# One matmul for centre and gate in two steps of eight, and one pair of PSUM buffers for both

## The chip, the cores and the metric

The kernel runs on one core of a Trainium2 chip. The metric is the device time of one execution in microseconds (us), lower is better. The engines are named as in the profile: PE is TensorE's matmul and PEld its weight load, DVE is VectorE, ACT is ScalarE, POOL is GpSimd, and SP issues DMAs. PE's results land in tiles of PSUM, which lie in banks, and DVE and ACT read them there. Everything is fp32.

## The reference, cut to what matters

The input `x` is an image of 512 x 512 pixels with 64 channels. Layer 0 is a triangle product with an output gate, layer 1 a spectral convolution; each is added to its input.

```python
xn  = _ln(x, norm_w, norm_b)                        # x is group-normed before
...
out_gate = sigmoid(xn @ ogate_w + ogate_b)          # (1, 512, 512, 64)
out = einsum('bkjd,bkid->bijd', left, right)        # masked and gated sides
out = _ln(out, onorm_w, onorm_b) @ out_w + out_b
x   = x + out * out_gate                            # layer 0
x   = x + ifft2(w * fft2(_gn(x))[12 x 12 modes])    # layer 1
```

The change is in `out_gate` alone. The kernel takes the layer norm in front of it apart: one matmul with `center_x` gives the centred pixels (their squares, summed over 64 channels, give the variance), another with `gate_x` gives the unscaled gate, and the gate is multiplied afterwards with the reciprocal standard deviation of its pixel.

## The kernel before, in words

Only at most 256 of the 512 rows are left by the mask, and the function `compact` works on those. After the statistics, the projections and the triangle product, it runs one long hand-ordered loop over steps `s` (L1193). Eight steps make a **unit** (`SIZE`). The first eight units (`k < first`) turn the triangle product into normed rows `u_d`; I call them the product stage. Then come 32 **output units**, `v = 0 .. 31`, each 128 rows by 64 pixels, and the change is about these. `manual_schedule` keeps every engine's instructions in the order of the source, and waits are put in from the tiles that instructions read and write.

In step `s`, with `n = s % 8`, the engines do this, in the order in which each has it:

- PE transposes four 128 x 128 blocks of step `s + 13` (`t_ps`, L1038), takes the gate of step `s` (`w_ps`, four matmuls of `times`, L1045) and then the centred pixels of step `s + 12` (`c_ps`, also L1045). In the steps with n = 0 and 4 the column transform (`f_ps`, L1140) follows. One fp32 matmul of the source is two instructions in the trace.
- ACT copies the transposed pixels to SBUF (`xt_c`, L1040); in even steps it takes the sigmoid of the gate that DVE finished in the step before (`z_t`, L1221); in the step n = 5 it takes the square root for the next unit (`rs_n`, L1089); last it squares the centred pixels of step `s + 12` (`sq_c`, L1076). In the trace one `ACT_TABLE_LOAD` stands ahead of the square root and one ahead of the next sigmoid.
- DVE takes four statistics of the finished unit (`stats2c`, L1168); in even steps it sums the squares of two steps (`scratch`, L1083); at n = 7 it takes the reciprocal of 64 standard deviations (L1263); then it multiplies the gate of step `s` with its factor (`z_t<-w_ps,rs_n`, L1274), and in odd steps it adds the gate's bias to the pair of steps (L1280). I write "multiplication(n)" and "add(n)" for the last two. In every fourth unit from v = 5 on, the steps n = 2 and 4 hold five more DVE instructions that join statistics (L1173 to L1186, and L230); I call these the join units.
- POOL multiplies the sigmoid with the normed row (L1109) and adds it to the pixels (L1113), each 128 x 1024 once in two steps, and issues two gathers a unit.

The PSUM tiles of the output stage are two buffers of one bank for `c_ps` and two of one bank for `w_ps`. They take the place of the two `y_ps` buffers (two banks each) of the product stage, which are closed when step 52 begins (L1206). In the product stage a tile `both` holds two 64 x 64 matrices beside each other in both halves of its partitions, and the matmul of L1058 takes 64 channels at a time, from the upper or the lower half: the results of a channel half are the centred pixels in the first 64 columns and the projected ones in the other 64. ACT squares the first (L1078) and copies the second to SBUF (L1079). `scratch` is one PSUM tile for sums of squares (`totals`), for the product stage's reciprocals (`factors`) and for biases.

## Time and profile before

| what | us |
|---|---|
| median of three runs (lowest, highest) | 1777.96 (1777.58, 1781.21) |
| the profiled execution, its time | 1777.78 |
| span of its trace, first to last instruction | 1776.0 |
| busy: PE, DVE, POOL, ACT | 1567.8, 1413.7, 936.5, 933.0 |
| product stage, first to last matmul of L1058 | 624.6 to 728.9 |
| first and last `c_ps` matmul | 730.5 to 1415.6 |
| first and last `w_ps` matmul | 747.8 to 1443.5 |

The chain of work that ended last is, from 1469 us to the end, the spectral layer and the DMAs that store the output; it does not reach back to the output units. So their pace is read from the trace itself: I cut it at the reciprocal that stands ahead of multiplication(7) (L1263), which gives one stretch for each unit. A line of the profile's groups gives the source line, the engine, what is written and read, the count, the busy time, the mean of one in ns, and behind the second bar the idle time of the engine just before them with what ended it. A line of the timeline gives start and duration in us, the engine, the line and, in brackets, the idle time before it.

### The profile page before, as it was taken

The page shows a single profiled execution, that of the slowest core. Times are in us where ns is not written, and L with a number is a line of the kernel's source. Part 1 is how long each engine was busy: PE and PEld are TensorE (multiplying, and loading weights), DVE is VectorE, ACT ScalarE, POOL GpSimd, SP SyncE. Part 2 cuts the span into 40 slices and gives each one's busy share as a digit, 9 for nine tenths or more (in the row PEclk, how much of TensorE's full clock was granted, in tenths as well). Part 3 has the DMA queues.
Part 4 walks back from the last instruction along what each step waited for, and adds up shares of the span by engine and source line. Part 5 has one row for each costly group of instructions (what it writes and reads, how often), then busy time and mean ns, then how long its engine had stood idle before and what let it go on. Part 6 is the DMA issues. An engine that isn't in the chain of part 4 may idle for free. (4 is left out here: it accounts for less than half of the span.)

```text
span 1776.0 us, 32619 instructions
## 1 busy us (share of the span) xinstructions
PE 1567.8 (88%) x10918; PEld 1242.0 (70%) x10918; DVE 1413.7 (80%) x2982; ACT 933.0 (53%) x1660; POOL 936.5 (53%) x695
## 2 busy tenths in 40 slices
PE   6779799997999978899999999999999977998772
PEld 5667666662899867787888888888888745665341
DVE  7989678887455568688999999999999984865451
ACT  3666566663333266676777777777777742011000
POOL 4666211111000037698999999999999881111110
PEclk9999999999899999899999999999999976555555
DMA  7999278878898789868767767776776699999999
GB/s 281 386 386 388 107 206 227 229 229 245 279 305 303 257 246 347 298 196 296 265 242 257 253 233 259 264 249 239 249 264 244 212 318 400 425 427 427 426 427 385
DMA packets 192593, 518.48 MB, mean 292 GB/s; under 512 B 37664, under 2 KB 104480, under 8 KB 151456
## 3 DMA queue, kind: packets, MB, share of 16 engines
q1 hardware_dynamic: 156112, 295.65, 47.5%
q0 software_dynamic: 32832, 218.45, 33.4%
q10 hardware_dynamic: 3472, 2.20, 0.5%
q8 instruction: 89, 1.46, 0.3%
q14 instruction: 88, 0.72, 0.1%
HBM read 311.60 MB, written 204.60 MB: 291 GB/s over the span
## 5 line engine op out<-in xcount | busy, mean ns | idle before, releaser
L1045 PE MATMUL w_ps<-gate_x,xt_c 128*128 128x128 f32 x2048 | 280.5, 281 | 30.0 <-DVE z_t L1274 28.6
L1113 POOL TENSOR_TENSOR places<-places,z_t 128x1024 f32<-128x1024 f32 x127 | 301.3, 2372 | 8.0
L1045 PEld LDWEIGHTS w_ps<-gate_x,xt_c 128*128 128x128 f32 x2048 | 252.0, 194 | 46.4 <-DVE z_t L1274 44.6
L1045 PE MATMUL c_ps<-center_x,xt_c 128*128 128x128 f32 x2048 | 277.0, 279 | 0.8 <-ACT xt_c L1040 0.4
L1045 PEld LDWEIGHTS c_ps<-center_x,xt_c 128*128 128x128 f32 x2048 | 252.8, 194 | 3.8 <-ACT xt_c L1040 3.0
L1440 PE MATMUL l_ps<-places,rinv 24*128 24x512 f32 x512 | 206.2, 1118 | 29.3 <-DVE places L1447 19.0
L1168 DVE BATCH_NORM_STATS2 stats2c<-places 128x6 f32<-128x128 f32 x1024 | 220.5, 278 | 9.9 <-POOL places L1113 9.9
L1083 DVE TENSOR_REDUCE scratch<-sq_c 128x16 f32<-128x1024 f32 x160 | 194.6, 1216 | 31.1 <-ACT sq_c L1078 16.1
L1221 ACT ACTIVATE z_t<-z_t 128x1024 f32<-128x1024 f32 x128 | 135.5, 1058 | 131.8 <-DVE z_t L1280 131.1
L1440 PEld LDWEIGHTS l_ps<-places,rinv 24*128 24x128 f32 x512 | 119.8, 302 | 110.8 <-DVE places L1447 56.9
L1278 POOL TENSOR_TENSOR z_t<-z_t,bias_row_out 128x1024 f32<-128x1024 f32 x32 | 75.6, 2363 | 226.3 <-PE y_ps L1058 202.1
L1040 ACT ACTIVATE xt_c<-t_ps,ab_xc 128x512 f32<-128x512 f32 x256 | 176.0, 688 | 11.5 <-PE t_ps L1038 10.6
L1274 DVE TENSOR_TENSOR z_t<-w_ps,rs_n 128x512 f32<-128x512 f32 x256 | 172.0, 672 | 6.2 <-PE w_ps L1045 6.1
L1076 ACT ACTIVATE sq_c<-c_ps 128x512 f32<-128x512 f32 x256 | 150.8, 589 | 31.4 <-PE c_ps L1045 30.8
L1280 DVE TENSOR_TENSOR z_t<-z_t,scratch 128x1024 f32<-128x1024 f32 x128 | 156.3, 1221 | 9.9 <-ACT rs_n L1089 3.7
L688 DVE BATCH_NORM_STATS2 stats1c<-x_ps 128x6 f32<-128x512 f32 x256 | 157.1, 682 | 7.7 <-PE x_ps L687 7.4
L1109 POOL TENSOR_TENSOR z_t<-z_t,places 128x1024 f32<-128x1024 f32 x64 | 151.8, 2371 | 14.6 <-ACT z_t L1221 14.4
L1038 PE MATMUL t_ps<-c_ident,places 128*128 128x128 f32 x1024 | 158.4, 278 | 0.0
L1038 PEld LDWEIGHTS t_ps<-c_ident,places 128*128 128x128 f32 x1024 | 118.5, 142 | 51.4 <-issue 51.4
L1447 DVE TENSOR_TENSOR places<-places,l_ps 128x512 f32<-128x512 f32 x176 | 109.3, 682 | 55.2 <-DMA places<-x_h,dst_i 42.1
L1109 POOL TENSOR_TENSOR z_t<-z_t,bias_row_out 128x1024 f32<-128x1024 f32 x63 | 149.4, 2372 | 5.8 <-ACT z_t L1221 5.5
L673 ACT COPY xc<-xg 128x128 f32 x352 | 105.0, 298 | 66.1 <-POOL xc L673 47.1
(214 smaller groups left out, 2557.0 us busy)
## 6 DMA issues: line engine op xcount, KB each, us to landing
x_h<-places SPq DMA_DIRECT2D x64, 1024.0 KB
out_x<-places SPq DMA_DIRECT2D x44, 1024.0 KB
places<-u_d SPq DMA_DIRECT2D x512, 64.0 KB
out_x<-lx_t SPq DMA_DIRECT2D x20, 1024.0 KB
rbc<-rs_d POOLq DMA_DIRECT2D x32, 512.0 KB, 7.1
left_d<-o_c SPq DMA_DIRECT2D x64, 256.0 KB
right_d<-o_c SPq DMA_DIRECT2D x64, 256.0 KB
left_raw<-left_d SPq DMA_DIRECT2D x64, 256.0 KB
```

What stands on the lines that cost most here:

```text
L688: nc.vector.bn_stats(stats[:, 0, 16 * (jc % quarter) + 4 * r + c, :], ps.rearrange("p i k -> p (i k)"))
L1038: nc.tensor.transpose(tps[:, i, :], flat[:, o : o + P], ident)
L1040: nc.scalar.activation(xts[s], tps, AF.Identity, bias=ab1[:, 2:3])
L1045: nc.tensor.matmul(ps[:, 2 * i : 2 * i + 2, :], xts[s][:, i, :], w, start=True, stop=True)
L1076: nc.scalar.activation(sq, cps, AF.Square)
L1083: nc.vector.tensor_reduce(totals[k % 2][:, 8 * (n - 1) : 8 * (n + 1)], sqs.pop(s // 2), AX.X, ALU.add)
L1109: nc.gpsimd.tensor_mul(zs[k, c], zs[k, c], u)
L1113: nc.gpsimd.tensor_add(xr, xr, zs.pop((k, c)))
L1168: nc.vector.bn_stats(st[k // 4][:, g, k % 4, :], x_of(k)[:, :, 2 * g : 2 * g + 2])
L1274: nc.vector.tensor_mul(z[:, 8 * odd : 8 * odd + 8, :], wps, rs)
L1280: nc.vector.tensor_add(z, z, bias_ps["ogate"].unsqueeze(1).to_broadcast([P, 16, C]))
L1440: nc.tensor.matmul(ps.rearrange("p j o -> p (j o)"), rinv[h, b, :], it[h], start=True, stop=True, tile_position=(32 * g, 0),)
```

## The change

The tile `both`, which only the product stage used, is filled a second time when step 52 begins: the two diagonal blocks of `center_x` and of `gate_x`. In the output units, the steps with `s % 4 == 0` (n = 0 and 4) are called joint. For a joint step the centred pixels and the gate come from eight matmuls of 64 channels each, at the place where the centred pixels alone were made, that is 12 steps before the gate is needed. ACT squares the centred half and copies the gate half to SBUF, over the transposed pixels. Twelve steps later DVE reads the gate from there.

The other six steps make the centred pixels and the gate with the same matmuls as before, in the same order. But the `y_ps` buffers now stay open: each step takes one tile of two banks, with the centred pixels of step `s + 12` in the first bank and the gate of step `s` in the second. There are two such tiles.

The reciprocals of a unit are taken in two instructions: 16 of them, for the joint steps, go to `factors` in the PSUM tile `scratch`, and 48 stay in SBUF. The multiplication of a joint step so reads its gate from SBUF and its factor from PSUM; in the other steps it is the other way round, as before.

```diff
+                    def joint(s):
+                        return s >= first * SIZE and s % 4 == 0
+                    def times(bank, s, w):
                         for i in range(4):
+                            nc.tensor.matmul(bank[:, i, :], xts[s][:, i, :], w, start=True, stop=True)
+                        return bank.rearrange("p i (h c) -> p (i h) c", h=2)
...
+                    def centered(s, ps):
+                        if joint(s):
+                            for i in range(4):
+                                for h in range(2):
+                                    hs = slice(h * C, (h + 1) * C)
+                                    nc.tensor.matmul(ps[:, h, i, :], xts[s][hs, i, :], both[hs], start=True, stop=True)
+                            return ps
                         if s >= first * SIZE:
-                            return times(ps_c, "c_ps", s, center_x)
+                            return times(ps[:, 0], s, center_x)
...
-                        if s >= first * SIZE:
+                        if joint(s):
+                            nc.scalar.activation(in_order(sq), cps[:, :, :, :C], AF.Square)
+                            kept = xts[s].rearrange("p i (h c) -> p (i h) c", h=2)
+                            nc.scalar.copy(in_order(kept), cps[:, :, :, C:])
+                        elif s >= first * SIZE:
                             nc.scalar.activation(sq, cps, AF.Square)
...
                         if s + LEAD - 1 == first * SIZE:
-                            products.close()
-                            ps_c = products.enter_context(tc.tile_pool(name="np_c", bufs=2, space=PSUM))
-                            ps_w = products.enter_context(tc.tile_pool(name="np_w", bufs=2, space=PSUM))
+                            for h in range(2):
+                                hs = slice(h * C, (h + 1) * C)
+                                nc.vector.tensor_copy(both[hs, :C], center_x[hs, hs])
+                                nc.vector.tensor_copy(both[hs, C:], gate_x[hs, hs])
+                        if s + LEAD - 1 >= 0 and s < total_g:
+                            ps = ps_y.tile([P, 2, 4, P], F32, name="y_ps")
                         if 0 <= s < total_g:
-                            wps = raw(s) if k < first else times(ps_w, "w_ps", s, gate_x)
+                            if k < first:
+                                wps = raw(s)
+                            elif joint(s):
+                                wps = xts[s].rearrange("p i (h c) -> p (i h) c", h=2)
+                            else:
+                                wps = times(ps[:, 1], s, gate_x)
...
-                            nc.vector.reciprocal(factors[(k + 1) % 2] if k + 1 < first else rss[k + 1], rss[k + 1])
+                            if k + 1 < first:
+                                nc.vector.reciprocal(factors[(k + 1) % 2], rss[k + 1])
+                            else:
+                                by = [t.rearrange("p (a b) -> p a b", a=2) for t in (factors[(k + 1) % 2], rss[k + 1])]
+                                nc.vector.reciprocal(by[0][:, :, :8], by[1][:, :, :8])
+                                nc.vector.reciprocal(by[1][:, :, 8:], by[1][:, :, 8:])
...
-                                rs = rss[k][:, 8 * n : 8 * n + 8].unsqueeze(2).to_broadcast([P, 8, C])
+                                rs = (factors[k % 2] if joint(s) else rss[k])[:, 8 * n : 8 * n + 8]
+                                rs = rs.unsqueeze(2).to_broadcast([P, 8, C])
```

The function `finished`, which multiplies the last two gates of all in PSUM, takes one `y_ps` tile in place of two `c_ps` tiles.

More of the change, by code (lines that the diff above doesn't have):

```diff
@@ L996, in compact @@
                     ps_y = products.enter_context(tc.tile_pool(name="np_b", bufs=2, space=PSUM))
-                    ps_c = ps_w = None
                     both = lp.tile([P, P], F32, name="both")
@@ L1040, in transpose @@
                         nc.scalar.activation(xts[s], tps, AF.Identity, bias=ab1[:, 2:3])
-                    def times(pool, name, s, w):
-                        ps = pool.tile([P, 8, C], F32, name=name)
+                    def joint(s):
+                        return s >= first * SIZE and s % 4 == 0
+                    def times(bank, s, w):
                         for i in range(4):
-                            nc.tensor.matmul(ps[:, 2 * i : 2 * i + 2, :], xts[s][:, i, :], w, start=True, stop=True)
-                        return ps
-                    def centered(s):
+                            nc.tensor.matmul(bank[:, i, :], xts[s][:, i, :], w, start=True, stop=True)
[7 more added lines that the diff above has]
+                            return ps
                         if s >= first * SIZE:
-                            return times(ps_c, "c_ps", s, center_x)
-                        ps = ps_y.tile([P, 2, 4, P], F32, name="y_ps")
+                            return times(ps[:, 0], s, center_x)
                         q, e = divmod(s, 2)
@@ L1064, in raw, with in_order @@
                         return xts[s].rearrange("p h (i c) -> p (h i) c", c=C).rearrange("p (h i) c -> p h i c", h=2)
+                    def in_order(t):
+                        return t.rearrange("p (i h) c -> p h i c", h=2)
                     def of_pair(t, e):
@@ L1117, in finished @@
                         z = zs.pop((last, 3))
-                        made = [ps_c.tile([P, 8, C], F32, name="c_ps") for _ in range(2)]
+                        made = ps_y.tile([P, 2, 4, P], F32, name="y_ps")
+                        made = [made[:, i].rearrange("p i (h c) -> p (i h) c", h=2) for i in range(2)]
                         for i, ps in enumerate(made):
@@ L1206, in compact @@
                         if s + LEAD - 1 == first * SIZE:
-                            products.close()
-                            ps_c = products.enter_context(tc.tile_pool(name="np_c", bufs=2, space=PSUM))
-                            ps_w = products.enter_context(tc.tile_pool(name="np_w", bufs=2, space=PSUM))
-                        if 0 <= s < total_g:
-                            wps = raw(s) if k < first else times(ps_w, "w_ps", s, gate_x)
-                            del xts[s]
+                            for h in range(2):
[4 more added lines that the diff above has]
+                            ps = ps_y.tile([P, 2, 4, P], F32, name="y_ps")
+                        if 0 <= s < total_g:
+                            if k < first:
[4 more added lines that the diff above has]
+                                wps = times(ps[:, 1], s, gate_x)
                         if 0 <= s + LEAD - 1 < total_g:
-                            cps = centered(s + LEAD - 1)
+                            cps = centered(s + LEAD - 1, ps)
                         if n in (0, 4) and held(1):
@@ L1287, in compact @@
                                     zs[v, c] = z
+                        xts.pop(s, None)
                         if n == 7 and held(0) and v < last:
```

## The prediction

> **What bounds the kernel now.** The change touches only the output units, so I read their stretch. On the profile's page I look at the two operations that meet there, PE's gate matmul and DVE's multiplication, and at the idle time behind their second bar.

> ```profile
> L1045 PE MATMUL w_ps<-gate_x,xt_c 128*128 128x128 f32 x2048 | 280.5, 281 | 30.0 <-DVE z_t L1274 28.6
> ...
> L1274 DVE TENSOR_TENSOR z_t<-w_ps,rs_n 128x512 f32<-128x512 f32 x256 | 172.0, 672 | 6.2 <-PE w_ps L1045 6.1
> ```

> PE waits 28.6 us for DVE to give a gate buffer back; DVE waits 6.1 us for PE. So DVE leads and PE follows, although PE's busy share is the higher one. Next I cut the trace at each reciprocal and ask for the busy times of the units (three plain units and a join unit; columns: stretch, length, busy time of each engine):

> ```profile
> 880.94:901.92 20.98, 20.72 (x178) 18.30 (x177) 20.77 (x51) 16.10 (x25) 20.43 (x11) 1.00 0.65 244
> 901.92:922.89 20.97, 20.84 (x178) 18.29 (x177) 20.76 (x50) 15.88 (x24) 20.43 (x10) 1.00 0.77 261
> 922.89:943.87 20.98, 20.72 (x178) 18.30 (x177) 20.77 (x51) 16.10 (x25) 20.42 (x11) 1.00 0.67 251
> 943.87:967.76 23.89, 21.92 (x176) 19.49 (x175) 23.15 (x56) 16.66 (x26) 21.98 (x12) 0.93 0.66 200
> ```

> PE, DVE and POOL all look full. DVE is: a plain unit holds 49 DVE instructions back to back, with no gap over 0.11 us. POOL is close: by the distance of equal gathers it needs about 21.4 us a unit, 0.4 more than DVE's 20.97, and catches up in the join unit. PE's share is a pile of overlapping records: its matmuls start 0.112 us apart, so a step costs 16 x 0.112 + 4 x 0.109 = 2.23 us and a unit about 20. Only ACT (16 of 21 us) has room. So in this stage **whatever DVE waits or does more is added to the time**, up to what POOL already lags.

> Last I read ACT and DVE instruction by instruction, in the steps n = 4 to 7 of one unit. DVE first: add(3), then reduction(4), multiplication(4), multiplication(5), add(5), reduction(6) and multiplication(6).

> ```profile
> 913.28 1.22 DVE L1280 TENSOR_TENSOR z_t<-z_t,scratch 128x1024 f32<-128x1024 f32 x1
> ...
> 915.20 1.21 DVE L1083 TENSOR_REDUCE scratch<-sq_c 128x16 f32<-128x1024 f32 x1
> 916.32 0.68 DVE L1274 TENSOR_TENSOR z_t<-w_ps,rs_n 128x512 f32<-128x512 f32 x1
> ...
> 917.70 0.67 DVE L1274 TENSOR_TENSOR z_t<-w_ps,rs_n 128x512 f32<-128x512 f32 x1
> 918.48 1.22 DVE L1280 TENSOR_TENSOR z_t<-z_t,scratch 128x1024 f32<-128x1024 f32 x1
> ...
> 921.52 0.68 DVE L1274 TENSOR_TENSOR z_t<-w_ps,rs_n 128x512 f32<-128x512 f32 x1
> ```

> And ACT beside it:

> ```profile
> 914.60 1.06 ACT L1221 ACTIVATE z_t<-z_t 128x1024 f32<-128x1024 f32 x1 [1.94 <-DVE z_t L1280]
> 915.56 0.58 ACT L1076 ACTIVATE sq_c<-c_ps 128x512 f32<-128x512 f32 x1
> 916.04 0.68 ACT L1040 ACTIVATE xt_c<-t_ps,ab_xc 128x512 f32<-128x512 f32 x1
> 916.74 1.28 ACT L1089 ACT_TABLE_LOAD   x1
> 918.03 0.31 ACT L1089 ACTIVATE rs_n<-scratch,eps 128x64 f32<-128x64 f32 x1
> 918.24 0.59 ACT L1076 ACTIVATE sq_c<-c_ps 128x512 f32<-128x512 f32 x1
> 918.72 0.69 ACT L1040 ACTIVATE xt_c<-t_ps,ab_xc 128x512 f32<-128x512 f32 x1
> 919.78 1.28 ACT L1221 ACT_TABLE_LOAD   x1 [0.36 <-DVE z_t L1280]
> 921.07 1.06 ACT L1221 ACTIVATE z_t<-z_t 128x1024 f32<-128x1024 f32 x1
> 922.04 0.58 ACT L1076 ACTIVATE sq_c<-c_ps 128x512 f32<-128x512 f32 x1
> ```

> See two things. Every sigmoid waits for an add, about 0.09 us after its end, so ACT starts afresh every two steps and carries no backlog. And the Square of step 5 ends at 918.83, **1.13 us after multiplication(5) has started**; that of step 6 ends at 922.62, 1.10 us after multiplication(6). Today nobody minds.

> **The change, part by part.**

> *The new wait.* I read the built program's list of waits. Before, the multiplication of the gate waits for its `w_ps` matmuls. After, in the six steps that are not joint, it waits for ACT's Square of the same step: gate and centre lie in one `y_ps` tile, and the reader of one half is ordered behind the reader of the other. Behind the waiting multiplication, in DVE's queue, stand its add, the next statistics and the next reduction; for the add waits the next sigmoid, and POOL behind that. Taken from the rows, counted from the add before:

> - n = 5: ACT's chain is sigmoid, Square(4), copy(4), `xt_c`, table load, square root, Square(5). It ends 918.83 - 913.28 = 5.55 us after the add's start, plus the new copy. The copy's price by the product stage's copies of the same shape: 0.59 us alone, 0.48 from its start to the next instruction's (915.56 to 916.04, the Square's spacing). I take 0.48. With 0.04 for the semaphore (Square end to reduction start in the product stage) the multiplication may start at 6.07; today it starts at 4.42. Late by 1.65; the add loses its present 0.07 of waiting for the square root, which is then long done. **+1.58.** In the join units DVE has 0.75 us more to do at n = 4 (the rows 0.49 and 0.26): +0.9.
> - n = 6: add, table load, sigmoid, Square(6): 922.62 + 0.04 against 921.52. **+1.14.**
> - n = 1, 2, 3, 7: today's Square ends, with the copy where it is ahead, and multiplication starts, both after the add's start: n = 1 4.5 against 4.4 (covered by the item below), n = 2 2.90 against 3.04, n = 3 3.96 against 4.42, n = 7 5.24 against over 6. Nothing, by a margin of 0.14 at n = 2.

> *The joint steps on DVE.* The factor now comes from `scratch`, which the reduction just ahead writes; the list of waits has DVE wait for its own reduction. The product stage has this pair: the multiplication starts 1.32 us after the reduction (730.00 to 731.32), in the output units 1.12 (915.20 to 916.32). +0.20 at n = 0; at n = 4 it is swallowed by the wait at n = 5. The multiplication itself costs the same (L1271, SBUF and PSUM swapped: 686 ns against 672 to 678). **+0.20.**

> *The split reciprocal.* One more instruction. Its fixed part by the spacing of 512 and 1024 elements: 0.598 - (1.138 - 0.598) = 0.06 us; at most 0.19, the spacing of the statistics. **+0.06**.

> *PE.* Two row halves run together: the product stage starts matmuls of 64 channels in pairs 0.007 us apart, a pair every 0.112.

> ```profile
> 669.81 1.84 PE L1058 MATMUL y_ps<-both,places 64*128 64x128 f32 x28
> ...
> 917.63 1.06 PE L1045 MATMUL w_ps<-gate_x,xt_c 128*128 128x128 f32 x8
> ```

> So a joint step takes 0.9 us in place of 1.8, 1.8 a unit. PE's stretch is shorter, but PE is not what DVE waits for, except 6.1 us in all; these go. If the halves did not overlap, PE would need 20 of 24 us and the forecast would stand.

> *Copies to `both`.* Four 64 x 64 copies, once, ahead of a reduction that waits for ACT's Square in a stretch where DVE is idle 5.03 us: nothing.

> The sum per plain unit: 1.58 + 1.14 + 0.20 + 0.06 = **2.98 us**, so 20.97 becomes 23.95. POOL's 21.4 is then cover no more, but slack. Over the stage:

> - 15 plain units (three of them with 0.47 us of columns): 15 x 2.98 = 44.7.
> - The three after these, which now wait for PE and the square root (21.72, 21.72, 23.35): to 23.95, +5.1.
> - Seven join units: 0.20 + 0.90 + 1.14 + 0.06 = 2.30 each, less 0.3 in four that wait for the square root today: +14.9.
> - v = 1 to 4: 92.6 us, of which DVE waits about 7 for POOL (3.2 in v = 1, 3.7 in v = 3). A DVE 12 us later finds POOL done, I think: four units of 23.95, less 0.6 in v = 1, which begins without statistics. +2.6.
> - v = 0 has no statistics to hide ACT's chain: its step pairs become 3.6 + 4.7 + 6.7 + 6.0 = 21.0 in place of 16.6: +4.4.
> - From n = 4 of v = 30 on there is no centre, hence no Square to wait for: +0.2.

> Together **+71.9 us**. The tail behind the stage is bound by its stores and starts that much later. Against the profiled execution (1777.78, span 1776.0; the median of the runs is 1777.96) that gives 1849.7, said as **1850 us**.

> [...]

> **The rivals.**

> - *PE sets the pace (faster).* Its busy column is the fullest. If that were the bound, each of 30 units would lose 1.8 us: 1778 - 54 = 1724. It decides where DVE waits for PE; the rows show 6.1 us of that against 28.6 the other way. 4%.
> - *The Square is always there in time.* Then DVE pays only its own 0.20 + 0.20 + 0.06 for 31 units, 14.3, less 6.1: 1786. Against it: the Squares at n = 5 and 6 end 1.1 us late already today. 7%.
> - *The wait spreads.* Multiplication, gate, centre, Square, multiplication is now a ring over two steps: 0.68 + 0.1 + 1.95 + 0.04 + 0.59 + 0.04 = 3.4 us, against 5.1 that DVE needs. If ACT is later than I count by the 0.14 to 0.5 us of margin at n = 1, 2 and 3, each unit loses up to 1 us more: 1880. 7%.

> **How the numbers follow.** The forecast has 82%, and its own bounds are 1833 (the copy hidden in ACT's idle time and no wait at n = 0: 2.3 a unit) and 1872 (half a microsecond more a unit, and the 7 us of POOL waits stay). I give 1832 to 1872, which leaves out the rivals. A measurement of this kernel tells 0.2%, 3.6 us, from no change: faster 0.04, same 0.01, slower 0.95.

> **What would show it.** Right: DVE's multiplication waits for ACT's Square with some 1.6 us at n = 5 and 1.1 at n = 6 in each unit, about 75 us in all; plain units of 24 us; PE idle. Wrong: units of 21 us, or waits at n = 1 to 3; or POOL's waits still there.

## The result and the profile after

The changed kernel takes **1862.18 us** (median of five runs, 1859.7 to 1864.06) against 1777.96 (five runs, 1776.11 to 1783.76): ratio 1.0468, 95% interval 1.0448 to 1.0488, slower. The forecast was 1850, the range 1832 to 1872. The profiled execution has a span of 1860.4, 84.4 more than before.

First the same groups as before, from the page of the changed kernel (behind the second bar: idle time of the engine just before the group, and what ended it).

```profile
L1046 PE MATMUL y_ps<-gate_x,xt_c 128*128 128x128 f32 x1536 | 212.6, 283 | 26.9 <-DVE z_t L1302 25.4
...
L1302 DVE TENSOR_TENSOR z_t<-y_ps,rs_n 128x512 f32<-128x512 f32 x192 | 129.5, 674 | 82.1 <-ACT sq_c L1090 82.0
...
L1054 PE MATMUL y_ps<-both,xt_c 64*128 64x128 f32 x1024 | 87.5, 316 | 100.6 <-DVE z_t L1302 100.6
```

DVE's 6.1 us of waiting for PE are gone, and the same multiplication now waits 82.0 us for ACT's Square. One multiplication still takes 674 ns. PE sits idle for 100.6 us ahead of the joint matmuls, and what ends that is DVE. Next the units, cut as before (two plain units, a join unit, a plain unit; stretch, length, busy time of PE, PEld, DVE, ACT, POOL, then the granted clock).

```profile
823.73:847.66 23.93, 19.36 (x181) 16.55 (x180) 21.19 (x51) 16.59 (x26) 20.83 (x11) 1.00 0.74 245
847.66:871.59 23.93, 19.36 (x181) 16.55 (x180) 21.18 (x52) 17.08 (x27) 20.84 (x11) 1.00 0.63 223
871.59:897.36 25.77, 20.66 (x181) 17.15 (x180) 23.56 (x57) 17.22 (x28) 20.89 (x11) 0.93 0.70 244
897.36:921.77 24.41, 20.66 (x178) 17.16 (x177) 21.28 (x51) 17.18 (x27) 20.82 (x11) 0.92 0.53 179
```

A plain unit is 23.93 where 20.97 was, and DVE's busy time has grown by 0.41 of these 2.96 us: the rest is waiting. The fourth row is a plain unit too, at 24.41, with a granted clock of 0.92; that difference comes up again below. Last DVE and ACT in the steps n = 4 to 6 of one unit (start, duration, and in brackets the idle time and what ended it):

```profile
958.02 1.22 DVE L1308 TENSOR_TENSOR z_t<-z_t,scratch 128x1024 f32<-128x1024 f32 x1
...
961.18 0.69 DVE L1302 TENSOR_TENSOR z_t<-xt_c,scratch 128x512 f32<-128x512 f32 x1
...
964.09 0.69 DVE L1302 TENSOR_TENSOR z_t<-y_ps,rs_n 128x512 f32<-128x512 f32 x1 [1.44 <-ACT sq_c L1090]
...
968.98 0.69 DVE L1302 TENSOR_TENSOR z_t<-y_ps,rs_n 128x512 f32<-128x512 f32 x1 [1.04 <-ACT sq_c L1090]
```

```profile
959.34 1.06 ACT L1243 ACTIVATE z_t<-z_t 128x1024 f32<-128x1024 f32 x1 [1.94 <-DVE z_t L1308]
960.30 0.58 ACT L1086 ACTIVATE sq_c<-y_ps 128x512 f32<-128x512 f32 x1
960.78 0.57 ACT L1088 COPY xt_c<-y_ps 128x512 f32<-128x512 f32 x1
961.24 0.70 ACT L1038 ACTIVATE xt_c<-t_ps,ab_xc 128x512 f32<-128x512 f32 x1
961.96 1.28 ACT L1103 ACT_TABLE_LOAD   x1
963.26 0.31 ACT L1103 ACTIVATE rs_n<-scratch,eps 128x64 f32<-128x64 f32 x1
963.47 0.59 ACT L1090 ACTIVATE sq_c<-y_ps 128x512 f32<-128x512 f32 x1
```

The Square of n = 5 ends at 964.06, and multiplication(5) starts 0.03 us later, 6.07 after the add at 958.02: the number that the prediction worked out. ACT's chain from sigmoid to Square runs without a gap, so this is ACT's own length and nothing that ACT waits for.

**Where the 84.4 us lie.** Summed over the stretches of both traces: the stretch of v = 0 starts 5.1 later (753.08 against 747.97); v = 0 itself +5.6; v = 1 to 4 +3.7; v = 5 to 29 +70.1 (619.72 against 549.59), of which the seven join units are +15.5; v = 30 +0.8; all behind it -0.9.

### The profile page after: what moved, and what is told of

The parts are those of the page before. It is cut to its first block, busy times and chain, and to the rows that moved or that the text cites. A ratio compares the mean times of both kernels' runs of the same rounds, so it can differ in the third digit from the quotient of the medians.

```text
span 1860.4 us, 32687 instructions
## 1 busy us (share of the span) xinstructions
PE 1549.2 (83%) x10918; PEld 1200.1 (65%) x10918; DVE 1427.1 (77%) x3018; ACT 959.2 (52%) x1724; POOL 936.4 (50%) x695
## 5 line engine op out<-in xcount | busy, mean ns | idle before, releaser
L1046 PE MATMUL y_ps<-gate_x,xt_c 128*128 128x128 f32 x1536 | 212.6, 283 | 26.9 <-DVE z_t L1302 25.4
L1046 PEld LDWEIGHTS y_ps<-gate_x,xt_c 128*128 128x128 f32 x1536 | 192.4, 197 | 39.7 <-DVE z_t L1302 33.7
L1097 DVE TENSOR_REDUCE scratch<-sq_c 128x16 f32<-128x1024 f32 x160 | 194.5, 1216 | 28.7 <-ACT sq_c L1092 25.3
L1046 PE MATMUL y_ps<-center_x,xt_c 128*128 128x128 f32 x1536 | 204.6, 277 | 0.0
L1302 DVE TENSOR_TENSOR z_t<-y_ps,rs_n 128x512 f32<-128x512 f32 x192 | 129.5, 674 | 82.1 <-ACT sq_c L1090 82.0
L1046 PEld LDWEIGHTS y_ps<-center_x,xt_c 128*128 128x128 f32 x1536 | 188.4, 193 | 0.6 <-ACT xt_c L1038 0.3
L1054 PE MATMUL y_ps<-both,xt_c 64*128 64x128 f32 x1024 | 87.5, 316 | 100.6 <-DVE z_t L1302 100.6
L1054 PEld LDWEIGHTS y_ps<-both,xt_c 64*128 64x128 f32 x1024 | 74.7, 215 | 113.7 <-ACT xt_c L1038 90.7
```

The lines of the kernel that those rows point to most:

```text
L1046: nc.tensor.matmul(bank[:, i, :], xts[s][:, i, :], w, start=True, stop=True)
L1054: nc.tensor.matmul(ps[:, h, i, :], xts[s][hs, i, :], both[hs], start=True, stop=True)
L1097: nc.vector.tensor_reduce(totals[k % 2][:, 8 * (n - 1) : 8 * (n + 1)], sqs.pop(s // 2), AX.X, ALU.add)
```

## The experiments

The theory: DVE waits for ACT because both read halves of one tile, and the later reader in program order is put behind the earlier one; the joint steps, copies and split factors cost little. The rivals: the joint steps or the copies are the cost, or the buffers as such. All edits are to the changed kernel unless it is said otherwise; each ratio is to the kernel before, run on the same chip.

**1. The shared tile alone.** The kernel before, with one two-bank tile for a step's centre and gate, and nothing else of the change:

```diff
-                            wps = raw(s) if k < first else times(ps_w, "w_ps", s, gate_x)
+                            wps = raw(s) if k < first else times(ps[:, 1], s, gate_x)
...
-                            return times(ps_c, "c_ps", s, center_x)
+                            return times(ps[:, 0], s, center_x)
```

> The kernel before, with one thing of the change alone: gate and centre of a step lie in one two-bank tile, of which there are two. No joint steps, no copies, one reciprocal. Theory (DVE's multiplication is ordered behind ACT's Square of the same tile): per plain unit 1.10 us more at n = 5 (Square ends 1.13 + 0.04 late, less 0.07) and 1.14 at n = 6, so 23.2 us a unit, some 1829 us in all (1815 to 1840), and DVE idle for ACT's Square. Rival (the joint steps and ACT's copies are what costs): 1778, give or take 4.

Measured: 1861.43 (ratio 1.0474, 1.0449 to 1.0499). The group of the multiplications in its page (behind the second bar the waits):

```profile
L1271 DVE TENSOR_TENSOR z_t<-y_ps,rs_n 128x512 f32<-128x512 f32 x256 | 173.0, 676 | 95.3 <-ACT sq_c L1074 93.3
```

The sharing alone makes a slowdown as large as that of the whole change. That the two totals agree to 1 us is in part luck: here the waits at n = 1 come to 25.4 us, with the joint steps to 8.9, while the joint steps bring 4.4 us more of waits at n = 5 and 6.2 us more of DVE's busy time in the units. The 1861 is also 32 more than expected. About half of its plain units take the 23.2 of the expectation, the others 24.7 to 25.1, with 1.4 us more of DVE's wait at n = 1. Experiments 11 and 12 take that up.

**2. The whole change, but separate banks.** Joint steps, copies and split factors stay; centre and gate get a one-bank tile each, and a joint step takes one of each:

```diff
-                        ps = ps_y.tile([P, 2, 4, P], F32, name="y_ps")
+                        ps = [pool.tile([P, 4, P], F32, name=name) for pool, name in ((ps_c, "c_ps"), (ps_w, "w_ps"))]
...
-                            nc.scalar.copy(in_order(kept), cps[:, :, :, C:])
+                            for h in range(2):
+                                nc.scalar.copy(in_order(kept)[:, h], cps[h][:, :, C:])
```

> The changed kernel with everything but the shared tile: centre and gate in two pools of two one-bank tiles, as in the kernel before; a joint step takes one tile of each, so ACT squares and copies it in two halves. Theory: DVE no longer waits for a Square; what stays is DVE's own 0.46 us a unit (two waits for its own reduction, one more reciprocal), 14 us, less the 6 us that DVE waited for PE: 1786 (1780 to 1795). Rival (joint steps and copies cost): 1850 or more.

Measured: 1792.63 (ratio 1.0072, 1.0051 to 1.0094). 70 of the 84 us are gone with the shared tile, and the multiplication waits for no Square. The 6 us above the expectation stand in another row of its groups:

```profile
L1315 DVE TENSOR_TENSOR z_t<-z_t,scratch 128x1024 f32<-128x1024 f32 x128 | 156.3, 1221 | 17.0 <-ACT rs_n L1105 12.4
...
L1309 DVE TENSOR_TENSOR z_t<-w_ps,rs_n 128x512 f32<-128x512 f32 x192 | 128.5, 670 | 2.6 <-PE w_ps L1046 2.4
```

The add of the bias waits for ACT's square root, 0.48 in each plain unit. It does not use the result: it reads the bias row in the tile `scratch`, and the square root reads the sums in the same tile. That is the mechanism of the change once more, in a tile that was there before.

**3 and 4. The Square earlier in ACT's order.** First ahead of sigmoid and square root in every step, then ahead of the square root at n = 5 alone (the second as a diff):

```diff
-                        if n == 5 and 0 <= k + 1 < first + len(units):
-                            root(k + 1)
                         if cps is not None:
                             squared(s + LEAD - 1, cps)
+                        if n == 5 and 0 <= k + 1 < first + len(units):
+                            root(k + 1)
```

> The changed kernel with its shared tile and its waits, but ACT issues the Square (and the copy) of a step ahead of the sigmoid and of the square root. Theory: the Square then is done before DVE asks, at n = 5 by 1.0 us and at n = 6 by more; the wait stays in the program and costs nothing: 1786 (1780 to 1798). Rival (the two shared buffers tie PE to both readers, or the joint steps cost): within 5 us of 1862.

> The changed kernel, but at n = 5 ACT issues the Square ahead of the square root and its table load; nothing else moves. Theory: the wait at n = 5 goes (1.5 us a plain unit, 0.75 a join unit), the one at n = 6 stays at 1.1: about 40 us less than the changed kernel, 1822 (1815 to 1832). Rival (the wait is set by PE or by the buffers, not by ACT's queue): within 5 us of 1862.

Measured: 1817.68 (ratio 1.0215, 1.0195 to 1.0236) and 1850.9 (ratio 1.0417, 1.0385 to 1.0449). Both are faster than the changed kernel, as a wait for ACT's order must be, and both miss the number expected. In the second the wait at n = 5 is gone (two units keep 1.2 and 1.3 us of it), and one that was hidden behind it appears (DVE's timeline, n = 5 and 6):

```profile
960.43 1.22 DVE L1308 TENSOR_TENSOR z_t<-z_t,scratch 128x1024 f32<-128x1024 f32 x1 [0.84 <-ACT rs_n L1103]
964.59 0.69 DVE L1302 TENSOR_TENSOR z_t<-y_ps,rs_n 128x512 f32<-128x512 f32 x1 [1.03 <-ACT sq_c L1090]
```

The square root, now behind the Square, holds the add for 0.84. In the first, 20.7 us of waits for the Square and 13.0 for the square root are left.

**5. The readers turned round.** `squared` stands behind DVE's multiplication in the source, so that the Square waits for the multiplication:

```diff
-                        if cps is not None:
-                            squared(s + LEAD - 1, cps)
...
                         if wps is not None:
...
+                        if cps is not None:
+                            squared(s + LEAD - 1, cps)
```

> The changed kernel with the order of the two readers of a tile turned round: in the program ACT's Square stands behind DVE's multiplication, so that Square waits for the multiplication and the multiplication waits for PE alone. Theory (the cost is DVE's wait on Square, 82.0 us in the changed kernel): those waits go; the wait of the gate's add for the square root, as with separate banks, may come in their place (0.25 to 0.48 us a unit): about 1792, within 1786 to 1800. Rival (the shared buffers themselves are the cost, however the readers are ordered, since PE's next matmuls then wait for a later Square): 1840 or more, the wait now standing at PE.

Measured: 1806.21 (ratio 1.0137, 1.0112 to 1.0162), 6 above the bounds of the theory and 34 below the rival's. The buffers are still shared, and 56 of the 84 us are gone: it is the order of the two readers. The same group in its page, no longer with a wait for the Square:

```profile
L1300 DVE TENSOR_TENSOR z_t<-y_ps,rs_n 128x512 f32<-128x512 f32 x192 | 128.7, 670 | 15.5 <-PE y_ps L1046 15.3
```

What is left: DVE's multiplication waits 15.3 us for PE, its add 8.8 for the square root and 3.3 for another ACT instruction of the join units.

**6. One reciprocal, all factors in SBUF** (on top of experiment 5):

```diff
-                                rs = (factors[k % 2] if joint(s) else rss[k])[:, 8 * n : 8 * n + 8]
+                                rs = rss[k][:, 8 * n : 8 * n + 8]
```

> As the kernel with the multiplication first, and also one reciprocal as before the change, with all factors in SBUF: the multiplication of a joint step then reads both operands from SBUF, and nothing in it waits for DVE's own reduction. Theory (two small terms of the prediction, 0.20 and 0.06 us a unit, 0.10 and 0.05 by the rows): 4 to 8 us below the kernel with the multiplication first. Rival (a DVE multiplication with both operands in SBUF holds POOL up, and POOL has little to spare in this stage): no gain, POOL's multiplications longer than their 2.36 us and DVE waiting for POOL.

Measured: 1906.4 (ratio 1.0712, 1.0692 to 1.0731), 100 us above experiment 5. The theory of a small gain is wrong, and the rival right, though it named the wrong victim. The group's mean (ns, ahead of the second bar) and one of its instructions beside POOL:

```profile
L1295 DVE TENSOR_TENSOR z_t<-xt_c,rs_n 128x512 f32<-128x512 f32 x64 | 174.4, 2725 | 0.0
```

```profile
904.50 2.85 DVE L1295 TENSOR_TENSOR z_t<-xt_c,rs_n 128x512 f32<-128x512 f32 x1
```

```profile
904.43 2.37 POOL L1123 TENSOR_TENSOR z_t<-z_t,places 128x1024 f32<-128x1024 f32 x1
906.87 2.68 POOL L1127 TENSOR_TENSOR places<-places,z_t 128x1024 f32<-128x1024 f32 x1
```

With gate and factor both in SBUF the multiplication takes 2725 ns, with one of them in PSUM 687. It starts 0.07 us after POOL's and ends 0.55 after POOL's end; POOL's next one takes 2.68 in place of 2.37. Among all 64 this is sharp: 63 of them end 0.54 to 0.56 us after the end of a POOL instruction, whenever they started, and the one that met no POOL instruction takes 683 ns. Two a unit cost 2 x 2.04 = 4.1 us; a plain unit takes 25.48 in place of 21.58, and v = 0 to 30 together 97.6 us more. Why the two hold each other up, no row says. So the change's split of the reciprocal, which looks clumsy, is what keeps its joint steps cheap.

**7. One copy more.**

```diff
                             nc.scalar.copy(in_order(kept), cps[:, :, :, C:])
+                            nc.scalar.copy(in_order(kept), cps[:, :, :, C:])
```

> The changed kernel with the copy of a joint step's gate made twice; nothing else differs. Theory (DVE's wait at n = 5 is the end of ACT's chain, in which the copy stands): the wait at n = 5 grows by the spacing of one copy, 0.48 us, in each of some 28 units, and that at n = 1 by up to as much: 1874 to 1888. Rival (the wait is set by PE or by the buffers, and ACT has slack): 1862, within 4.

Measured: 1894.04 (ratio 1.0635, 1.0612 to 1.0659), 6 above the theory's bounds. ACT and DVE at n = 4 and 5:

```profile
944.60 0.58 ACT L1088 COPY xt_c<-y_ps 128x512 f32<-128x512 f32 x1
945.21 0.59 ACT L1089 COPY xt_c<-y_ps 128x512 f32<-128x512 f32 x1
945.69 0.69 ACT L1038 ACTIVATE xt_c<-t_ps,ab_xc 128x512 f32<-128x512 f32 x1
```

```profile
948.53 0.69 DVE L1303 TENSOR_TENSOR z_t<-y_ps,rs_n 128x512 f32<-128x512 f32 x1 [2.05 <-ACT sq_c L1091]
```

The two copies start 0.61 apart, and the wait goes from 1.44 to 2.05, by 0.61. At n = 1 a wait of 0.35 to 0.43 appears. So the chain of ACT ahead of the Square sets the wait, term by term. Of the 31.4 us in span, 25.6 lie in the units and 4.8 behind the last one (see "Nothing ahead of the output units" in the next section).

**8 to 10. Sums of squares in SBUF.** Experiment 2 named the tile `scratch`. So its sums get tiles of their own, first with separate banks (run twice), then in the kernel before, without anything of the change:

```diff
-                    totals = [scratch[:, i, : SIZE * 8] for i in range(2)]
+                    totals = [lp.tile([P, SIZE * 8], F32, name=name) for name in ("tot_0", "tot_1")]
```

> The kernel with separate banks for centre and gate (1792.6), and the sums of squares in SBUF tiles of their own, apart from the bias row and the factors in the scratch bank. Theory (the gate's add waits for ACT's square root only because both read the scratch tile, 12.4 us in that kernel, and the joint multiplication waits for the reduction only because that writes it, 2.1 us): both waits go, a plain unit falls from 21.70 to about 21.13, the whole to about 1778 (1774 to 1784). Rival (the square root is awaited for another reason, or a reduction from SBUF to SBUF holds POOL up): 1790 or more.

> The kernel before the change, with nothing but the sums of squares moved into SBUF tiles of their own. It tells what part of the 1776.8 of the kernel with separate banks and such sums comes from the change's joint steps. Theory (joint steps buy nothing, since DVE and POOL set the pace and PE follows; before, the gate's add waits 0.07 us a unit for the square root in plain units, and 0.3 to 0.5 in the three after the columns): 1772 to 1780, the same as that kernel within 4. Rival (PE's shorter joint steps are worth something once DVE waits less for it): 1780 or more, at least 4 above that kernel.

> The kernel with separate banks and the sums of squares in SBUF once more, beside the kernel before with such sums on one chip: 1776.8 within 4.

Measured: 1776.76 (ratio 0.9978, 0.9966 to 0.9990) and 1777.18 (0.9984, 0.9973 to 0.9995) with the joint steps; 1772.61 (ratio 0.9959, 0.9945 to 0.9973) without. The row of the adds in the second of them:

```profile
L1315 DVE TENSOR_TENSOR z_t<-z_t,scratch 128x1024 f32<-128x1024 f32 x128 | 156.3, 1221 | 4.9
```

The wait for the square root is gone, and a reduction from SBUF to SBUF is no slower (1207 ns against 1216). With this and separate banks the changed kernel is 0.2% faster than the kernel before, but the kernel before with the same edit is 0.4% faster, the fastest of all. Its units v = 0 to 30 take 673.0 us, those with joint steps 676.6 (675.0 in the second trace): of the 3.6 us more, 0.13 lies in each unit behind a join unit, 0.4 in each third unit behind one (with 0.27 of waiting for POOL) and 0.75 in each of two behind the columns (0.78 of waiting for PE in place of 0.20). What causes these was not looked for; the split reciprocal costs 0.01 (0.46 to the next multiplication in place of 0.45). The two medians lie 4.2 and 4.6 apart, a little more than the 4 of the theory, on the side away from the rival: PE's shorter steps are worth nothing here.

**11 and 12. Keeping PE busy.** Where do the units of 24.7 in experiment 1 and of 24.4 in the changed kernel come from? The starts of three plain units of experiment 1 (7 us each, the last but two the granted clock):

```profile
892.25:899.25 7.00, 7.00 (x63) 6.04 (x62) 6.93 (x16) 3.52 (x6) 6.27 (x4) 1.00 0.10 37
915.47:922.47 7.00, 7.00 (x49) 5.59 (x48) 5.58 (x14) 3.04 (x6) 6.25 (x4) 0.76 0.65 203
940.42:947.42 7.00, 7.00 (x63) 6.04 (x62) 6.93 (x16) 3.52 (x6) 6.26 (x4) 1.00 0.35 133
```

The units that start at 892.25 and 940.42 take 23.2, the one at 915.47 takes 24.96. That holds for all plain units from v = 2 on: a long one has a clock below 0.9 at its start, a short one 1.00. In the changed kernel, finer, around the start of the unit at 897.36:

```profile
892.00:894.00 2.00, 2.00 (x20) 2.00 (x19) 2.00 (x6) 1.05 (x1) 1.09 (x2) 1.00 0.60 254
894.30:896.60 2.30, 0.21 (x2) 0.00 (x0) 1.26 (x3) 2.30 (x4) 1.22 (x1) 1.00 0.90 274
898.00:900.00 2.00, 2.00 (x9) 0.34 (x10) 1.97 (x5) 0.35 (x1) 2.00 (x1) 0.50 0.35 139
901.00:904.00 3.00, 3.00 (x29) 3.00 (x29) 2.51 (x7) 2.43 (x5) 2.92 (x2) 1.00 0.00 0
```

PE is busy for 0.21 of 2.30 us, waiting for DVE; afterwards its clock stands at 0.50 for about 3.4 us. An idle time of 2.15 us did it here, while one of 2.50 ahead of the unit at 847.66 did not. The traces show what sets the two apart. In those of the kernel before and of the changed kernel all stretches of lower clock, 17 and 38, start on one grid of 3.413 us, to 0.001 us. Two windows of that grid around each of the two idle times (PE's busy time first, the clock last but two):

```profile
894.11:897.52 3.41, 1.26 (x19) 1.05 (x18) 2.37 (x8) 3.30 (x6) 2.14 (x1) 1.00 0.97 329
897.52:900.94 3.42, 3.42 (x20) 1.53 (x17) 3.39 (x8) 1.29 (x2) 2.74 (x3) 0.50 0.34 137
842.91:846.32 3.41, 1.55 (x14) 1.31 (x13) 2.37 (x7) 3.06 (x4) 1.83 (x3) 1.00 1.01 423
846.32:849.74 3.42, 2.78 (x30) 1.86 (x31) 3.39 (x9) 1.41 (x3) 3.34 (x2) 1.00 1.02 410
```

The idle time of 2.15 lies in one window, and the clock is halved in the next; that of 2.50 is cut by the grid into 1.86 and 0.64. In the units of the changed kernel, 22 windows at full clock hold 1.99 us of PE's idle time or more, and the clock falls after each of them; of those with 1.90 or less it falls after two alone, which hold the 24 short matmuls of a column transform (128x24, PE not idle). In the kernel before, from 748 to 1440 us, it falls after windows with 1.88, 1.90, 1.91 and 1.97 us (twice) and after one with those 24 matmuls, and not after another with 1.90. To test that the fall makes the unit long, the centre matmuls of the step n = 7 are issued three times, first in experiment 1's kernel, then in the changed one; the two extra rounds write the same values:

```diff
+                            for _ in range(2 if (s + 5) % SIZE == 0 and s < total_g - 1 else 0):
+                                times(ps[:, 0], s, center_x)
                             return times(ps[:, 0], s, center_x)
```

> The kernel with nothing but the shared tile (1861.4), and the centre matmuls of the step n = 7 issued three times instead of once into the same half: 1.8 us of idle work for PE, in the 2.3 us in which it sits waiting for DVE ahead of the next unit. Theory (the units of 24.7 in place of 23.2 are those in which the granted clock falls to 0.5 for some 3.5 us after that idle time, so that the Square at n = 1 is late): the clock stays at 1.00 at the units' starts, nearly all plain units take 23.2, and some 14 units save 1.5 us: about 1840 (1834 to 1848), faster for doing more. Rival (PE's lateness there is queueing, or the falls of the clock have nothing to do with PE's idle time): 1861 or more.

> The changed kernel with the same three centre matmuls at n = 7. Theory: PE's 2.5 us of idle time ahead of the joint matmul shrink to 0.7, the clock no longer falls there, and the waits at n = 1 go: 0.4 us in each of 12 units and 1.8 us in one join unit, some 6 us: 1856 (1853 to 1859). Rival (the waits at n = 1 have another cause): 1862 or more.

Measured: 1848.63 (ratio 1.0385, 1.0358 to 1.0413) and 1860.26 (ratio 1.0440, 1.0421 to 1.0459). The starts of the same three units in experiment 11:

```profile
893.03:900.03 7.00, 7.00 (x63) 6.04 (x62) 6.93 (x16) 3.52 (x6) 6.28 (x4) 1.00 0.27 107
916.26:923.26 7.00, 7.00 (x63) 6.04 (x62) 6.93 (x16) 3.52 (x6) 6.26 (x4) 1.00 0.64 201
939.69:946.69 7.00, 7.00 (x63) 6.04 (x62) 6.93 (x16) 3.53 (x6) 6.27 (x4) 1.00 0.37 136
```

The clock stays up, the unit in the middle takes 23.43, and the units v = 0 to 30 together 742.6 in place of 761.5, 18.9 less. It does not help everywhere: in three units behind the columns the extra matmuls make the Square itself late, and multiplication(7) waits 2.47, 2.47 and 0.84 for it (v = 12 and 20 take 26.31 in place of 23.22). In experiment 12 every plain unit without columns from v = 3 to v = 26 takes 23.93 or 23.94, the unit v = 13 takes 25.77 in place of 27.63, and the units give 5.1 back. So the units get shorter by giving PE more to do, and in the traces the theory stands. The medians fall by 12.8 and 1.9 only, which ends 0.6 and 1.3 us above the theory's bounds, and the 1.9 is within the scatter of the runs: in these two traces 4 to 5 us more lie behind the last unit, and in experiment 11 the first unit starts 4.6 later.

## Why the prediction was right, and where it was off

- *DVE sets the pace, and what it waits is added.* Right. The units grew by 80.2: DVE's idle times over 0.15 us went from 17.0 to 82.1 (82.0 of these for the Square; those for PE, POOL and the square root are gone), its busy time grew by 13.0, the small gaps by 2.1.
- *The new wait.* Right in mechanism and size: 1.44 at n = 5 (1.65 forecast; the start, 6.07 after the add, is the forecast one, and part of the delay is the joint multiplication's own), 1.04 at n = 6 (1.14), 82.0 in all (75). Experiments 1, 2 and 5 show that the shared tile and the order of its readers make it, experiment 7 that its size is the end of ACT's chain.
- *Self-wait and split reciprocal.* The joint multiplication starts 1.24 to 1.33 after its reduction, where 1.32 was forecast; the split costs 0.01 a unit where 0.06 was counted. Both small, as said.
- *Plain unit 23.95, join unit 2.30 more.* 23.93, and seven join units 15.5 more in place of 14.9; that this sum is so near is luck, since 1.8 of it is the wait at n = 1 of v = 13, and the other six units grew by 1.9 to 2.1 each, 11.8 together.
- *n = 1: nothing.* **This step failed.** In 12 of the 18 plain units from v = 6 on the multiplication at n = 1 waits 0.2 to 0.4, in the join unit v = 13 1.76: 4.5 and 1.8 us. The prediction had put it at nothing, since "PE is not what DVE waits for", and did not count that PE comes back from its idle time with a lower clock (0.50 from 897.52 on, after 2.15 us) and is then late in the ring that the third rival describes. Experiments 11 and 12 show the cause. That rival had the place right, but gave ACT's margin as the reason.
- *v = 0.* 5.6 in place of 4.4: 22.24 against 21.0, the Square waits there being 7.3 in all. v = 1 to 4: 3.7 in place of 2.6; v = 30: 0.8 in place of 0.2. DVE's waits for POOL in the units, 7.4 before, are gone, as forecast. With these, the 71.9 of the forecast fall 12.5 short of the 84.4 measured: 5.1 ahead of the units, 5.4 in v = 5 to 29, 2.9 in the other units, less 0.9 behind them.
- *Nothing ahead of the output units.* Off by 5.1, and not settled. The product stage's first matmul starts 1.6 us later, its last one ends 5 us later. The same kernel run twice (experiments 8 and 10) has v = 0 start at 747.9 and 750.7, so a part is scatter from run to run. The stretch behind the last unit varies likewise from 347 to 355 us among all these traces; why is open.
- *Tile and order.* With separate tiles (experiment 2) the multiplication waits for no Square, and with the tile still shared and its readers turned round (experiment 5) for none either. So the wait comes from the program, which orders readers by tile; a tile each for centre and gate, or the other order, took it away. `scratch` is another case: its sums and its bias row lie in one tile, and it was moving the sums to SBUF that parted them; the add's wait for the square root, 12.4 us in experiment 2, is then gone.
- *The rivals.* "PE sets the pace" is out: PE's idle times in the units went from 26.9 to 125.1 us. "Always in time" comes near with separate tiles, at 1792.6 against 1786.

## What to carry to other kernels

Before two buffers are merged, look at who reads each half: here a second reader on another engine was put behind the first, and a pace-setting engine took over the lag of an idle one. Separate tiles in separate banks (1792.63 us), or the pace-setter first in program order (1806.21), took the 82.0 us of waiting for the Square away. Relief for an engine that already follows bought nothing here (PE's shorter steps: 1776.76 and 1777.18, without them 1772.61), and where a long chain of waits was cut, the next one (the bias in `scratch`, 12.4 us) showed at once.
